# Layer norms inside an attention layer: the row scaling moved two pairs ahead of the transposes

## The chip, the cores and the metric

The kernel runs on one core of a Trainium2 chip. Its metric is the device time of one launch in microseconds (us), as the median of several runs. Engines are called as the profile calls them: PE is TensorE, with PEld for its weight loads; DVE is VectorE, ACT is ScalarE, POOL is GpSimd, and SP is SyncE, on whose queue the DMAs are issued.

## The reference, cut to what matters

Two layers work on 8 images of 256 channels and 32 x 32 positions. Layer 0 is a convolutional attention with a feed-forward part. Its output is read as 8 sequences of 1024 tokens with 256 channels each. Layer 1, where the change lies, is:

```python
t = _to_tokens(x)
t = t + _L1_attn_ref(_ln_t(t), WQ, WK, WV)
t = t + _L1_ffn_ref(_ln_t(t), ...)

def _ln_t(v, eps=1e-5):
    m = jnp.mean(v, axis=-1, keepdims=True)
    s = jnp.var(v, axis=-1, keepdims=True)
    return (v - m) / jnp.sqrt(s + eps)

def _L1_attn_ref(E, WQ, WK, WV):
    ...
    W = jnp.einsum('bqd,bkd->bqk', Q, K) / scale
    M = jnp.where(W == 0, jnp.zeros_like(W), tril[None, :, :])
    x_exp = jnp.exp(W - x_max) * M
    A = x_exp / (jnp.sum(x_exp, axis=-1, keepdims=True) + EPS)
    return jnp.einsum('bqk,bkd->bqd', A, V)
```

So every image passes two layer norms: a first one ahead of its attention and a second one behind it. The feed-forward part is a mixture of 8 experts; its gate reads the mean of the normed tokens over the images.

## The kernel before, in words

The launch has three stages: layer 0 (0 to some 1424 us), layer 1's attention (to some 2077 us), and the mixture of experts, called MoE here (to the end).

In layer 1 an image t[b] lies with its channels on the partitions, as two halves of 128 channels (KC = 2) by 1024 tokens. A norm over the channels needs tokens on the partitions, so `layer_norm` (L1287) turns the image, norms its rows, and turns them back. It works on n blocks of 128 tokens in pairs. For each pair PE makes four transposes into one PSUM bank `tpt`, ACT copies them to `zt`, and DVE takes mean and variance (`bn_stats`, `bn_aggr`) into `mv`. When all pairs are done, six small POOL operations make the factors `r`. Then `scaled(i0)` (L1317) subtracts the mean from the rows of a pair and multiplies them with r, in place, by two DVE operations (zt<-zt,mv,r). Four transposes (`tpz`) and one ACT copy per pair bring them back into `dst`. `zt` is one buffer for all blocks (bufs=1), so no pair waits for room of another.

The order of the instructions on each engine is the order of the program: all engines are called through `InOrder` (L60), which records every instruction at L72, so that L72 is the line of all of them in the profile. The program interleaves generators. `together(main, side, ratio)` (L446) runs main; at each step main yields its estimated time, and the side gets steps as long as the sum of what it has yielded is below 0.85 of main's sum. What is left of the side when main has ended runs after it. The number behind a `yield` thus decides only how many steps of the other generator stand between two pieces of work.

For each image b the main generator is `causal(b)` (L1527): for each of 8 rows of 128 queries, `scores` (L1543; s<-kk,z in two halves, on DVE the negated maximum `nm`, on ACT the exponential into `pr`), and then `follow` (L1532), which issues what became ready: a `product` (L1584; po<-pT,v, then t<-t,po on DVE), the `norm` of a former row (L1559; DVE: the lower triangle, the sum, the reciprocal rs; POOL: pr<-pr,rs), and from the third row on the `turn` of a former row (L1570; transposes tp<-ident,pr of up to four blocks into one bank, with an ACT copy into pT). The last rows of an image are turned during the next image's first scores.

The side is `beside(b)` (L1601), in this order: `first_norm(b + 1)`, the norm of the next image into z; three steps of `chores`, the experts' weights cut into parts (DVE: parts_w); `second_norm(b - 1)`, the norm of the image before into z2, with the sums for the gate on POOL (feat<-feat,z, in two halves), and `z_parts` (L1505), which cuts z2 in parts for the MoE stage (ACT: parts, DVE: parts<-z,parts and z<-parts) and stores them; two more chores; `keys_values(b + 1)` (L1465; pk on PE copied by ACT to kk, pv copied to v); two more chores. Beside the last image stand `last_norm` (L1516, n = 4) and the gate's first half in place of keys_values. The MoE stage calls `layer_norm` once more in `last_half` (L1820, n = 4), which advances by two steps in every second of its rounds.

The banks `tpt`, `tpz` and `tp` share one tag of the PSUM pool ps_t with two buffers (`bank`, L1455, and L1577 of `turn`): a tile of one of these kinds waits for the ACT copy of the tile two before it in that order. Scores have two buffers of their own (ps_s); pk, pv and po share two more (ps_m).

Of the kernel before, what the change touches and what calls it, by code (L numbers as in the profile page):

```python
# [104 lines left out]
def conv_attn_hybrid_kernel(  # L105
# [1181 lines left out]
    def layer_norm(src, dst, zt, room, bank):  # L1287

        n = src.shape[2] // P
        mv = room([P, NT, 2], "mv", 2)  # L1290
        for i0 in range(0, n, 2):
            tp = bank([P, 2, C], "tpt")
            for i in range(2):
                for k in range(KC):
                    c0 = (i0 + i) * P
                    pe.transpose(tp[:, i, k * P : (k + 1) * P], src[:, k, c0 : c0 + P], ident)
            act.copy(zt[:, i0 : i0 + 2, :], tp)
            yield 0.6
            for i in range(i0, i0 + 2):
                st = room([P, 6], "st", 4)  # L1300
                dve.bn_stats(st, zt[:, i, :])
                dve.bn_aggr(mv[:, i, :], st)
            yield 0.6

        y = room([P, NT], "y1", 2)[:, :n]
        r = room([P, NT], "r1", 2)[:, :n]
        pool.tensor_scalar(y, mv[:, :n, 1], LN_EPS, None, ALU.add)
        pool.tensor_tensor(r, y, mhalf1[:, :n], ALU.pow)
        pool.tensor_mul(y, y, r)
        pool.tensor_mul(y, y, r)  # L1310
        pool.tensor_scalar(y, y, -0.5, 1.5, ALU.mult, ALU.add)
        pool.tensor_mul(r, r, y)

        for _ in range(4):
            yield 1.0

        def scaled(i0):  # L1317
            for i in range(i0, i0 + 2):
                dve.tensor_scalar(zt[:, i, :], zt[:, i, :], mv[:, i, 0:1], r[:, i : i + 1], ALU.subtract, ALU.mult)

        scaled(0)
        yield 0.5
        for i0 in range(0, n, 2):
            if i0 + 2 < n:
                scaled(i0 + 2)
            tp = bank([P, KC, 2, P], "tpz")
            for i in range(2):
                for k in range(KC):
                    pe.transpose(tp[:, k, i, :], zt[:, i0 + i, k * P : (k + 1) * P], ident)
            act.copy(dst[:, :, i0 * P : (i0 + 2) * P], tp.rearrange("p k i c -> p k (i c)"))  # L1330
            yield 0.9
# [31 lines left out]
    with ExitStack() as l1:  # L1363
# [88 lines left out]
        def room(shape, tag, bufs):  # L1452
            return tiny.tile(shape, F32, tag=tag, name=tag, bufs=bufs)

        def bank(shape, name):  # L1455
            return ps_t.tile(shape, F32, tag="tp", name=name)
# [4 lines left out]
        def first_norm(b):  # L1461
            z[b] = two.tile([P, KC, N], F32, tag="z", name="z1")
            yield from layer_norm(t[b], z[b], rows_of_zt(), room, bank)
# [25 lines left out]
        def second_norm(b):  # L1489
            yield from until((b, N // QC - 1))  # L1490
            z2 = two.tile([P, KC, N], F32, tag="z2", name="z2", bufs=1)
            yield from layer_norm(t[b], z2, rows_of_zt(), room, bank)
            nc.sync.dma_start(u_d[b], t[b])
            if b + 3 < B:
                load_t(b + 3)
            for h, feat in enumerate(feats):
                half = z2[:, :, h * HALF : (h + 1) * HALF]
                if b == 0:
                    pool.tensor_copy(feat, half)
                else:  # L1500
                    pool.tensor_add(feat, feat, half)
            for h in range(2):
                yield from z_parts(b, h, z2[:, :, h * HALF : (h + 1) * HALF])
# [12 lines left out]
        def last_norm():  # L1516

            yield from until((B - 1, HALF // QC - 1))
            yield from layer_norm(t[B - 1][:, :, :HALF], z2_last, rows_of_zt(), room, bank)
            dve.tensor_add(feats[0], feats[0], z2_last)  # L1520
            nc.sync.dma_start(u_d[B - 1][:, :, :HALF], t[B - 1][:, :, :HALF])
            yield 0.5
# [459 lines left out]
```

## Time and profile before

| what | us |
|---|---|
| median of 3 runs | 3204.36 |
| lowest and highest of them | 3199.16, 3207.84 |
| the profiled execution, whole | 3211.16 |
| its span, first to last instruction | 3209.1 |
| PE busy (92% of the span) | 2950.3 |
| DVE busy (74%) | 2380.9 |
| ACT busy (49%) | 1568.7 |
| POOL busy (11%) | 342.7 |

The mean granted clock of PE was 0.964 of full speed. One profiled execution lies behind every duration given later; its own time is 6.8 us above the median. A line of the timeline or of the groups of instructions names the engine, the operation, its output and inputs by the program's names, the shapes (partitions x elements), how many of them (x4), and in brackets the engine's idle time just before it, with what ended it. The start of a line and its length come first, in us. In the page's groups the two numbers behind the bar are the busy us of the group and the mean ns of one instruction. PE's instructions overlap by their pipeline, so the length of one includes some of the next.

### The profile page before, as it was taken

The page shows a single profiled execution, that of the slowest core. Times are in us where ns is not written, and L with a number is a line of the kernel's source. Part 1 is how long each engine was busy: PE and PEld are TensorE (multiplying, and loading weights), DVE is VectorE, ACT ScalarE, POOL GpSimd, SP SyncE. Part 2 cuts the span into 40 slices and gives each one's busy share as a digit, 9 for nine tenths or more (in the row PEclk, how much of TensorE's full clock was granted, in tenths as well). Part 3 has the DMA queues.
Part 4 walks back from the last instruction along what each step waited for, and adds up shares of the span by engine and source line. Part 5 has one row for each costly group of instructions (what it writes and reads, how often), then busy time and mean ns, then how long its engine had stood idle before and what let it go on. Part 6 is the DMA issues. An engine that isn't in the chain of part 4 may idle for free. (4 is left out here: it accounts for less than half of the span.)

```text
span 3209.1 us, 41633 instructions
## 1 busy us (share of the span) xinstructions
PE 2950.3 (92%) x16802; PEld 1936.8 (60%) x16802; DVE 2380.9 (74%) x3014; ACT 1568.7 (49%) x2312; POOL 342.7 (11%) x419
## 2 busy tenths in 40 slices
PE   5998898998998989958999999899999999999998
PEld 3654545554555555535566556577777777777776
DVE  1378778778787879574766665588988898888888
ACT  1554444454554546313333333365666666666665
POOL 1121212111111110001222221100000000000000
PEclk9998999999999999979999999899999999999999
DMA  5213030302121110011433221231211242221220
GB/s 151 60 22 79 27 80 27 79 27 69 38 63 44 52 42 8 17 58 57 150 116 118 105 102 53 109 121 66 99 66 66 73 162 100 92 73 66 86 79 27
DMA packets 63854, 234.85 MB, mean 73 GB/s; under 512 B 5590, under 2 KB 13862, under 8 KB 54822
## 3 DMA queue, kind: packets, MB, share of 16 engines
q1 hardware_dynamic: 63654, 232.12, 21.7%
q8 instruction: 134, 2.20, 0.3%
q14 instruction: 66, 0.54, 0.1%
HBM read 140.61 MB, written 91.49 MB: 72 GB/s over the span
## 5 line engine op out<-in xcount | busy, mean ns | idle before, releaser
L72 PE MATMUL pa<-ze,w 128*128 128x512 f32 x1488 | 422.8, 392 | 0.0
L72 DVE SCALAR_TENSOR_TENSOR x<-hpad,vec,x 128x1024 f32<-128x1024 f32 x248 | 317.1, 1283 | 40.6 <-ACT x L72 33.5
L72 DVE SCALAR_TENSOR_TENSOR conv<-hpad,vec,conv 128x1024 f32<-128x1024 f32 x256 | 329.3, 1293 | 15.5 <-ACT conv L72 8.9
L72 PEld LDWEIGHTS pa<-ze,w 128*128 128x128 f32 x1488 | 277.9, 188 | 63.2 <-issue 3.3
L72 ACT ACTIVATE h<-pa,bn_o,s1a 128x512 f32<-128x512 f32 x256 | 198.8, 777 | 207.3 <-PE pa L72 207.3
L72 ACT ACTIVATE pT<-s 128x1024 f32<-128x1024 f32 x256 | 247.5, 1025 | 72.0 <-PE s L72 72.0
L72 PE MATMUL po<-pT,vT 128*32 128x256 f32 x4096 | 273.4, 385 | 0.0
L72 PE MATMUL q<-h2p,w 128*128 128x512 f32 x768 | 269.4, 459 | 0.1
L72 DVE SCALAR_TENSOR_TENSOR h<-pa,s1b,h 128x512 f32<-128x512 f32 x256 | 191.4, 748 | 95.6 <-PE pa L72 87.0
L72 PE MATMUL s<-kk,z 128*128 128x512 f32 x512 | 247.9, 614 | 1.0 <-DVE pr L72 1.0
L72 PE MATMUL ph<-xn,piw 128*128 128x512 f32 x512 | 244.6, 615 | 3.1 <-DVE xn L72 1.6
L72 PE MATMUL pm<-h,w 128*128 128x512 f32 x512 | 240.9, 593 | 0.0
L72 PE MATMUL q<-z_first,w 128*128 128x512 f32 x768 | 216.5, 390 | 2.8 <-DVE z_first L72 1.7
L72 PE MATMUL pm<-h1p,w 128*128 128x512 f32 x768 | 217.0, 391 | 0.5 <-DVE h1p L72 0.5
L72 DVE SCALAR_TENSOR_TENSOR o<-vpad,pe_w,o 128x1024 f32<-128x1024 f32 x128 | 163.5, 1282 | 45.9 <-ACT o L72 42.7
L72 PEld LDWEIGHTS q<-h2p,w 128*128 128x128 f32 x768 | 144.5, 188 | 83.8 <-issue 59.6
L72 PE MATMUL s<-qst,kst 128*128 128x256 f32 x1024 | 176.1, 314 | 14.9 <-DMA kst<-part 13.5
L72 ACT ACTIVATE hpad<-ph,pi_o 128x512 f32<-128x512 f32 x126 | 86.9, 690 | 183.6 <-PE ph L72 183.6
L72 PEld LDWEIGHTS po<-pT,vT 128*32 128x32 f32 x4096 | 120.6, 110 | 85.6 <-issue 3.9
L72 PEld LDWEIGHTS s<-qst,kst 128*128 128x128 f32 x1024 | 137.6, 193 | 48.1 <-issue 42.7
L72 PEld LDWEIGHTS q<-z_first,w 128*128 128x128 f32 x768 | 144.2, 188 | 34.5 <-DVE z_first L72 2.9
L72 PEld LDWEIGHTS pm<-h1p,w 128*128 128x128 f32 x768 | 144.6, 188 | 32.1 <-DVE h1p L72 0.9
(268 smaller groups left out, 5065.7 us busy)
## 6 DMA issues: line engine op xcount, KB each, us to landing
ze<-zd SPq DMA_DIRECT2D x29, 1536.0 KB, 6.4
qst<-part SPq DMA_DIRECT2D x32, 512.0 KB, 8.6
kst<-part SPq DMA_DIRECT2D x32, 512.0 KB, 15.1
te<-ud SPq DMA_DIRECT2D x32, 512.0 KB, 4.1
wd<-parts_w SPq DMA_DIRECT2D x20, 768.0 KB, 3.6
w<-wd SPq DMA_DIRECT2D x20, 768.0 KB, 4.3
zd<-parts SPq DMA_DIRECT2D x14, 1024.0 KB, 4.1
t<-in_x_dram SPq DMA_DIRECT2D x8, 1024.0 KB, 5.2
```

The costliest lines, as they stand in the source:

```text
L72: return self._tc.keep_in_program_order(method(*args, **kwargs))
```

## The change

Only the second part of `layer_norm` is changed:

```diff
         scaled(0)
-        yield 0.5
+        yield 1.0
+        scaled(2)
+        yield 1.0
         for i0 in range(0, n, 2):
-            if i0 + 2 < n:
-                scaled(i0 + 2)
+            if i0 + 4 < n:
+                scaled(i0 + 4)
             tp = bank([P, KC, 2, P], "tpz")
             for i in range(2):
                 for k in range(KC):
                     pe.transpose(tp[:, k, i, :], zt[:, i0 + i, k * P : (k + 1) * P], ident)
             act.copy(dst[:, :, i0 * P : (i0 + 2) * P], tp.rearrange("p k i c -> p k (i c)"))
             yield 0.9
```

Before, the first pair was scaled, the generator yielded 0.5, and each turn of the loop scaled the next pair and then transposed its own. After it, the first pair is scaled, the generator yields 1.0, the second pair is scaled, it yields 1.0 again, and each turn scales the pair two further on and then transposes its own. The instructions are the same ones; a norm's yields add up to 1.5 more than before, and there is one more of them. All calls of `layer_norm` are affected: the first and second norms of the 8 images, last_norm, and last_half.

## Prediction

> **What bounds the kernel now.** I read the page's first two parts first, for the engine shares.
>
> ```profile
> PE 2950.3 (92%) x16802; PEld 1936.8 (60%) x16802; DVE 2380.9 (74%) x3014; ACT 1568.7 (49%) x2312; POOL 342.7 (11%) x419
> ```
>
> PE is busy 92% of the span. That is a mean over three stages, so the stage with the changed function was read alone. The changed code runs in layer 1's attention (about 1424 to 2077 us) and once, thinly spread, in the MoE stage. The table of windows for 80 us of the attention (columns: window, length, busy PE, PEld, DVE, ACT, POOL, clock, DMA share, GB/s):
>
> ```profile
> 1680.00:1760.00 80.00, 74.40 (x306) 47.67 (x305) 52.60 (x124) 27.40 (x48) 18.00 (x22) 0.98 0.34 131
> ```
>
> PE again 93%, DVE 66%, DMA a third: PE sets the pace, and a gap in PE is time. The waits from 1500 to 2000 us (six and a half images; columns: total us, times, longest) say where the gaps are:
>
> ```profile
> PE tpz L72 <- DVE zt L72: 21.6, 27, 1.5
> ...
> PE tp L72 <- ACT pT L72: 3.5, 6, 0.6
> PE pk L72 <- ACT kk L72: 2.1, 3, 0.7
> PE tp L72 <- ACT zt L72: 2.0, 6, 0.3
> ...
> PE tpz L72 <- ACT z L72: 1.4, 6, 0.2
> ```
>
> The norms' transposes (tpz) waiting for their scaled rows (zt) are the largest, some 3.3 us an image. The chain of waits at the end of the page covers only the last 37% of the span and is no help here. So I went through PE's timeline of one image. The first norm (of the next image):
>
> ```profile
> 1689.58 1.88 PE L72 MATMUL s<-kk,z 128*128 128x512 f32 x4
> 1692.31 0.67 PE L72 MATMUL tpz<-ident,zt 128*128 128x128 f32 x4 [0.85 <-DVE zt L72]
> ...
> 1695.80 0.66 PE L72 MATMUL tpz<-ident,zt 128*128 128x128 f32 x4 [0.24 <-ACT z L72]
> 1697.05 0.66 PE L72 MATMUL tp<-ident,pr 128*128 128x128 f32 x4 [0.59 <-ACT pT L72]
> ...
> 1699.70 0.59 PE L72 MATMUL s<-kk,z 128*128 128x512 f32 x1
> ```
>
> And the second norm (of the image before):
>
> ```profile
> 1719.01 3.60 PE L72 MATMUL s<-kk,z 128*128 128x512 f32 x8
> 1723.81 0.41 PE L72 MATMUL tpz<-ident,zt 128*128 128x128 f32 x2 [1.20 <-DVE zt L72]
> 1724.54 1.08 PE L72 MATMUL tpz<-ident,zt 128*128 128x128 f32 x6 [0.32 <-DVE zt L72]
> ...
> 1730.06 0.41 PE L72 MATMUL tpz<-ident,zt 128*128 128x128 f32 x2 [1.54 <-DVE zt L72]
> 1730.89 0.44 PE L72 MATMUL tpz<-ident,zt 128*128 128x128 f32 x2 [0.42 <-DVE zt L72]
> 1731.16 3.15 PE L72 MATMUL s<-kk,z 128*128 128x512 f32 x4
> 1734.11 3.66 PE L72 MATMUL po<-pT,v 128*128 128x256 f32 x16
> ```
>
> Records overlap, so I count from start to start: half a row of scores (4 records) holds PE 1.72 us, a tpz bank (4 transposes) 0.43, one tp transpose 0.11. The first norm's section runs from 1689.58 to about 1701.42 (1699.70 + 1.72), 11.84 us. Its work is 4 x 1.72 + 4 x 0.43 + 8 x 0.11 = 9.48, so 2.4 us are lost; the same section at 1535.71 to 1547.84 loses 2.65. The second norm's runs from 1719.01 to 1734.11, 15.1 us for 6.88 + 1.72 + 0.44 = 9.04 of work, so 6.1 are lost: 4.8 in waits, some 1.3 in the 3.15 us that the scores took instead of 1.88.
>
> [...] the windows of PE at the same place one image earlier show it busy all the time at half clock,
>
> ```profile
> 1651.00:1653.00 2.00, 2.00 (x3) 0.50 0.00 0
> ```
>
> behind some 3.3 us with only transposes and waits. It comes about once an image. [...] for zt: 0.40 us alone, but its pair below takes 1.31 beside POOL's scaling of pr (1729.78 for 0.91, POOL's timeline):
>
> ```profile
> 1729.52 1.31 DVE L72 TENSOR_SCALAR zt<-zt,mv,r 128x256 f32<-128x256 f32 x2
> ```
>
> **The change, part by part.** No instruction is added or removed; the 96 zt of 483 ns, the transposes and the copies stay. Two scaled pairs stand ahead of the first tpz instead of one, and the generator yields 2.0 instead of 0.5 ahead of it: 1.5 more of main's steps. The rows are in one zt buffer of all 8 blocks, so two pairs ahead need no room.
>
> *First norm, 7 times (images 1 to 7).* VectorE's order at its start is as before: six zt in a row, then nm(1). PE's becomes: both halves of scores(1), tpz0, tp of row 7 (two banks), half of scores(2), tpz1, tpz2, the other half, tpz3, po(3). Scores(1) 1689.58 to 1693.02. The zt end about 1693.8, but the first pair is ready at 1692.2: tpz0 to 1693.45, no wait. The second tp bank needs tpz0's bank, whose copy (588 ns) ends about 1694.25: a stall of 0.4. Then scores to 1696.4. The pT copies stand behind exp(1) on ACT, which waits for nm(1) (1.22, to 1695.1), and end at 1696.2 and 1696.8, as tpz1 and tpz2 want them. Scores to 1699.0, tpz3, po(3) at 1699.5 where it was 1701.42. Gain 1.9; with the section at 1535 it is 2.26. I take 2.1: 7 x 2.1 = 14.7 us. Ends: 1.5 and 2.4 (all of it).
>
> *Second norm, 7 times beside attention (images 0 to 6).* PE before: scores(5), tpz0, tpz1, tp(3), half of scores(6), tpz2, tpz3, other half, po(2). After: scores(5), tp(3), half of scores(6), tpz0, tpz1, other half, tpz2, tpz3, po(2). Removed: the 1.20 + 0.32 ahead of tpz0, since tp(3) starts at 1722.5 and scores(6) runs to 1724.8 over the zt. Added: tpz1 takes the bank of tp(3), whose copy stands on ACT behind exp(5); that waits for nm(5), now 1725.0 to 1726.2 behind four zt; exp 0.90, copy 0.58: 1727.8, a stall of 2.55. Queued behind tpz1 on PE is the other half of scores(6), and nm(6) waits for that. It ends 1729.9. The last two scaled pairs come after norm(5), where POOL scales pr (0.91) and then adds feat, which the trace has at
>
> ```profile
> L72 POOL TENSOR_TENSOR feat<-feat,z 128x1024 f32<-128x1024 f32 x10 | 23.5, 2367 | 0.0
> ```
>
> Its first half needs only z0 and z1 and can now start near 1730.05. [...] the last zt end at 1732.7 and po(2) starts at 1733.2; if zt get in first, at 1731.3. Before it was 1734.11 in images with the half clock here, 1732.88 in the others, mean 1733.5. So +0.3 or +2.2. Behind it VectorE's and ACT's chain to exp(7) and the keys is nearly as late (the third pk started at 1745.69 or 1744.86, by my count 1744.75 after), so little of the better end passes on. Matmul-free stretches are 3.5 and 3.2 us long (before 3.75 and 3.24), so I keep one half-clock phase an image[...]. I take +0.4, ends -1.0 and +1.6: 7 x 0.4 = 2.8 us.
>
> *Last image and end.* In image 7, nm(7) no longer stands behind parts and z (1.22 us each) on VectorE, so the wait of po(5) at 2045.9 (5.3 us) shrinks by up to 3. At the end, last_norm's second tpt moves into the last po, and its chain of stats 1.15, POOL 2.5 and zt reaches its tpz some 2 us later. Together +1, ends -2 and +3.
>
> *Moved without price.* The side's sum grows by 3.0 an image, to about 59 against the 41.4 that main lets through, so more of keys_values runs after main; it did so before, PE-dense there, nothing lost. The DMA issues behind the second norm (u, t(b+3), parts) shift by under 3 us on SP's queue; t(b+3) is wanted two images later. POOL's factors r stand ahead of all this. In the MoE stage the norm has n=4 and one yield more, so the second gate comes one slot later, long before its use: 0.
>
> *Sum:* 14.7 + 2.8 + 1 = 18.5 us. The profiled run took 3211.16 (span 3209.1 and 2.1 around it): 3192.7. It lies 6.8 above the median of the runs, 3204.36, which gives 3186.
>
> **Rivals.** A difference under 0.3% (9.6 us) can hardly be told from none here.
> 1. *Likeliest, 0.45:* as summed, 13 to 25 us gained, 3179 to 3191, 3186.
> 2. *The second norm gains too, 0.15:* [...] the half-clock phase goes. 14.7 + 7 x 1.6 + 1 + some half-clocks (up to 7 x 1.3) is 27 to 36: 3172. The trace's 28.5 us of waits listed above are the ceiling but for the clock. Against: nearly equal stretches.
> 3. *The gain is given back in part, 0.26:* the second norm loses 1 us each (7), the first gains 1.5 (10.5), the end loses 2: 1.5 us; up to 13 with milder losses. 3197.
> 4. *Slower, 0.14:* [...] the other three wait 2.4 us, tpz2 as well as tpz3 is late, po(2) stands at 1733.8. The stretch is then 3.9 us[...]: 2.0 late. The second feat then blocks parts' subtraction (2.22 beside feat, 1.22 alone, at 1657.8): 3.0 in all. 7 x (2.1 - 3.0) - 2 = -8.3: 3213. It decides from 2.1 us of loss per second norm. For it: zt's 1.31 above. Against: VectorE issues its four zt back to back, and the path wants only the last.
>
> **How the numbers follow.** Faster by over 0.3%: 0.45 + 0.15 + 0.06 of case 3 = 0.66. Within: 0.20 of case 3 and 0.02 of case 4 = 0.22. Slower: 0.12. The range is 3169 to 3208: below lies 0.05, above some 0.12.
>
> **What would show it.** Right: PE's waits for zt in the first norm near 0, a new wait of about 0.4 of tp for z, an image period some 2 us shorter (76.8 now), PE busy time unchanged. In the second norm a wait of tpz for pT of about 2.5, then one for zt under 2.7. Wrong: a stretch at half clock on po(2) in each image, zt pairs at over 2 us, or scores waiting for nm(1) in the first norm.

## The result, and the profile after

The changed kernel takes 3189.32 us (median of 6 runs, 3185.13 to 3194.78); the kernel before took 3206.98 in the 6 runs beside it. The ratio is 0.9947, with a 95% interval of 0.9937 to 0.9957: some 17 us faster, where 18.5 was worked out. For each experiment the kernel before was measured again (medians 3204.5 to 3206.9), and each ratio below is against those runs.

The profiled execution of the changed kernel took 3188.79 us, its span 3186.8. That is 22.3 less than the profiled one before, but not all of it is the change's: layer 0 ended 3.0 us earlier, with the same code. From PE's last operation ahead of layer 1 (votes) to the gate's first matmul (lg) it was 641.9 us before and 621.1 after. From there to the end 1143.2 and 1144.7.

PE's waits from 1500 to 2000 us, after (total us, times, longest; lines of other engines left out):

```profile
PE tpz L72 <- ACT pT L72: 13.6, 6, 2.3
...
PE tpz L72 <- DVE zt L72: 5.2, 4, 2.0
...
PE tp L72 <- ACT zt L72: 2.0, 6, 0.3
...
PE tp L72 <- ACT z L72: 1.4, 6, 0.2
...
PE tpz L72 <- ACT z L72: 0.8, 1, 0.8
PE pk L72 <- ACT kk L72: 0.5, 3, 0.2
```

The 21.6 us of waits for zt have become 5.2, and a new wait of 13.6 has come, six times 2.27: tpz for the bank of tp(3), which the pT copy frees. The sum of PE's waits went from 31.0 to 23.5. PE's timeline of a first norm, after:

```profile
1528.15 3.60 PE L72 MATMUL s<-kk,z 128*128 128x512 f32 x8
1531.59 0.60 PE L72 MATMUL tpz<-ident,zt 128*128 128x128 f32 x4
1532.03 0.60 PE L72 MATMUL tp<-ident,pr 128*128 128x128 f32 x4
1532.86 0.66 PE L72 MATMUL tp<-ident,pr 128*128 128x128 f32 x4 [0.24 <-ACT z L72]
1533.36 1.88 PE L72 MATMUL s<-kk,z 128*128 128x512 f32 x4
1535.08 1.04 PE L72 MATMUL tpz<-ident,zt 128*128 128x128 f32 x8
1535.95 1.88 PE L72 MATMUL s<-kk,z 128*128 128x512 f32 x4
1537.67 0.60 PE L72 MATMUL tpz<-ident,zt 128*128 128x128 f32 x4
1538.11 6.65 PE L72 MATMUL po<-pT,v 128*128 128x256 f32 x32
```

From 1528.15 to 1538.11 it takes 9.96 us for 9.48 of work; only the wait for tpz0's bank is left. And a second norm:

```profile
1703.29 3.60 PE L72 MATMUL s<-kk,z 128*128 128x512 f32 x8
1706.72 0.60 PE L72 MATMUL tp<-ident,pr 128*128 128x128 f32 x4
1707.39 1.95 PE L72 MATMUL s<-kk,z 128*128 128x512 f32 x4
1709.18 0.60 PE L72 MATMUL tpz<-ident,zt 128*128 128x128 f32 x4
1712.05 0.67 PE L72 MATMUL tpz<-ident,zt 128*128 128x128 f32 x4 [2.27 <-ACT pT L72]
1712.54 3.58 PE L72 MATMUL s<-kk,z 128*128 128x512 f32 x4
1715.93 0.63 PE L72 MATMUL tpz<-ident,zt 128*128 128x128 f32 x4
1716.95 0.67 PE L72 MATMUL tpz<-ident,zt 128*128 128x128 f32 x4 [0.40 <-DVE zt L72]
1717.46 3.20 PE L72 MATMUL po<-pT,v 128*128 128x256 f32 x16
```

The wait of 1.20 ahead of the first tpz is gone; 2.27 ahead of the second has taken its place. The section, from scores(5) to po(2), takes 14.17 us. Its half row of scores at 1712.54 runs at half clock, as the windows show (columns: window, length, PE busy, clock, DMA share, GB/s; the clock is 0.50):

```profile
1713.00:1715.00 2.00, 2.00 (x3) 0.50 0.00 0
```

Behind it the last rows arrive late. VectorE's four zt, and POOL's work beside them:

```profile
1713.15 3.98 DVE L72 TENSOR_SCALAR zt<-zt,mv,r 128x256 f32<-128x256 f32 x4
1717.05 1.21 DVE L72 TENSOR_REDUCE nm<-s 128x1 f32<-128x1024 f32 x1
```

```profile
1713.40 0.91 POOL L72 TENSOR_SCALAR pr<-pr,rs 128x768 f32<-128x768 f32 x1 [4.79 <-DVE rs L72]
1714.28 2.38 POOL L72 TENSOR_TENSOR feat<-feat,z 128x1024 f32<-128x1024 f32 x1
```

Four zt of 0.40 take 3.98 us. feat runs from 1714.28 to 1716.66, and only then do the last zt end.

So a second norm now has three delays on top of one another (bank, half clock, feat), and two of them hide each other. Image 1's second norm, from 1628.98, has no half clock (1.00 all along): its tpz2 stands 1.7 us earlier in the section, tpz3 waits the longer for zt,

```profile
1639.95 0.70 PE L72 MATMUL tpz<-ident,zt 128*128 128x128 f32 x4
1642.64 0.67 PE L72 MATMUL tpz<-ident,zt 128*128 128x128 f32 x4 [2.00 <-DVE zt L72]
```

and the section takes the same 14.17 us.

By section, in the profiles, over six images each (first norm of images 2 to 7, second norm of images 0 to 5; the third column runs from po(2) to the first pv, and holds 14.54 us of work):

| kernel | first norm | second norm | po(2) to pv |
|---|---|---|---|
| before | 11.84 to 12.13 | 13.87 and 15.1 in turn | 15.0 and 15.5 in turn |
| after | 9.95 to 9.99 | 13.53, then 14.17 | 14.5 to 15.0, once 16.2 |

The 15.1 are the second norms whose last half row of scores runs at half clock (in the 13.87 a phase falls earlier, beside waits); the 16.2 is the one image of the changed kernel in which such a phase fell on po(2). The first norms of images 2 to 7 give 11.6 us, the second norms of images 0 to 5 2.5, the third column 0.9. The beginning of layer 1 gives 4.6: 2.7 of them in image 1's first norm, where a phase at half clock went as well, and 1.2 in the transposes and keys ahead of it, which began at half clock before and which the edit does not touch. The rest of the 20.8, some 1.3, is in the last image.

### The profile page after: what moved, and what is told of

Same layout as the page of the kernel before. It is cut to its first block, busy times and chain, and to the rows that moved or that the text cites. A ratio compares the mean times of both kernels' runs of the same rounds, so it can differ in the third digit from the quotient of the medians.

```text
span 3186.8 us, 41632 instructions
## 1 busy us (share of the span) xinstructions
PE 2936.5 (92%) x16802; PEld 1934.3 (61%) x16802; DVE 2390.5 (75%) x3014; ACT 1567.0 (49%) x2312; POOL 340.3 (11%) x419
## 4 chain that ended last, share of the span: by engine, by line
PE 46%; DVE 6%; ACT 2%; issue 1%; DMA 0%; POOL 0%; SPq 0%; ACTq 0%; DVEq 0%; POOLq 0%
PE pm L72 12%; PE pa L72 11%; PE q L72 11%; PE s L72 4%; PE po L72 3%; PE pv L72 2%; PE pk L72 1%; DVE nm L72 1%; DVE zt L72 1%; DVE pr L72 1%; ACT pr L72 1%; PE tpz L72 1%; PE tpt L72 1%; DVE st L72 1%; PE tp L72 1%
## 5 line engine op out<-in xcount | busy, mean ns | idle before, releaser
L72 PE MATMUL s<-kk,z 128*128 128x512 f32 x512 | 241.3, 603 | 1.0 <-DVE pr L72 0.6
## 6 DMA issues: line engine op xcount, KB each, us to landing
kst<-part SPq DMA_DIRECT2D x32, 512.0 KB, 15.1
```

The lines of the kernel that those rows point to most:

```text
L72: return self._tc.keep_in_program_order(method(*args, **kwargs))
```

## The experiments

My theory after this, A: the gain is made in the first norms; in the second norms new waits eat most of what the old ones cost. Rivals: the second norms carry half (B); the scaling ahead does it rather than the delay (C); the bank is what limits a second norm (G).

**First norms alone.** A flag gives `first_norm` the new form and leaves the others in the old one:

```diff
-            yield from layer_norm(t[b], z[b], rows_of_zt(), room, bank)
+            yield from layer_norm(t[b], z[b], rows_of_zt(), room, bank, True)
```

> The change in the first norms alone; second norms, last_norm and last_half as before. Theory A (the gain is made in the first norms, some 1.9 us in each of images 2 to 7 and 2.7 in image 1, by leaving no transpose in front of its scaled rows): 12 to 15 us faster than before, all but a few us of the whole change. Rival B (the second norms carry half of it): 7 to 9 us faster.

Measured: 3190.51, ratio 0.9949 (0.9935 to 0.9963), 16 us. First norms take 9.95 us, as in the change. A bit above the numbers of A, and its interval, 12 to 21 us, holds them; B's lie outside.

**Second norms alone.** The same flag at `second_norm`.

> The change in the second norms alone (8 of them), all else as before. Theory A: a second norm gains 0.4 us in the mean, since the waits for zt that go come back as a wait for the bank of tp(3) and one for zt behind POOL's feat: 0 to 6 us faster, 3 likeliest. Rival B: 7 to 10 us faster.

Measured: 3202.99, ratio 0.9997 (0.9988 to 1.0005), nothing to be told. The low end of A; B is out. The two parts together (0.51% and 0.03%) make the change's 0.53%. The profile shows the second norms at 14.17 us (the first at 13.53), as in the change, but in three images of six a phase at half clock falls on po(2), and the stretch from po(2) to pv takes 16.2 us instead of 15.0. Over the six images the sections gained 2.5 us, and that stretch lost 1.6 again.

**The delay without the scaling ahead.**

```diff
         scaled(0)
         yield 1.0
-        scaled(2)
         yield 1.0
         for i0 in range(0, n, 2):
-            if i0 + 4 < n:
-                scaled(i0 + 4)
+            if i0 + 2 < n:
+                scaled(i0 + 2)
```

> The yields as in the change (1.0 and 1.0), but rows scaled only one pair ahead, as before. Theory A (in a first norm the delay alone does it: PE has two halves of scores ahead of the first transpose, and the third pair, scaled behind norm(1), is ready when its transposes are due): first norms as in the change, second norms 1 us worse than in the change (the second pair now stands behind norm(5) on VectorE, its transposes wait for it): 8 to 15 us faster than before, 11 likeliest. Rival C (scaling two ahead is what frees PE): 0 to 5 us faster.

Measured: 3190.43, ratio 0.9954 (0.9941 to 0.9968), 15 us. First norms 9.95 us: as A has it, and C is out. In the first norms the delay is the change. The second norms are at 15.13 (one at 15.85), 1.0 above the change, and there the second tpz waits 3.27 us for its scaled pair. But all six also have a phase at half clock behind that wait, where nothing hides it: in the one from 1704.79 half a row of scores takes 2.84 us from start to start instead of 1.72, and eight tpz 1.43 instead of 0.87. So the 1.0 is not the price of the later pair alone; what the second scaled pair is worth by itself is not shown.

**The scaling ahead without the delay.**

```diff
         scaled(0)
-        yield 1.0
         scaled(2)
-        yield 1.0
+        yield 0.5
```

> Rows scaled two pairs ahead, but with a single yield of 0.5 as before, so PE's order is that of before and VectorE does all eight zt in a row. Theory A: in the first norms nothing (the transposes wait for the first pair and for banks, as before); in a second norm the waits of 1.54 and 0.42 for zt behind norm(5) go, and pT's bank is waited for some 0.8 instead: 1.5 to 2 us each, in all 8 to 16 us faster, 13 likeliest. Rival D (without the delay the scaling ahead is worth nothing, since new waits take its place): 0 to 3 us faster.

Measured: 3206.49, ratio 1.0008 (1.0001 to 1.0014). My 13 us did not come; D has the number. But the sections show that D's place is wrong: the first norms are as before (11.83), and the second norms did shrink, to 12.26 us, by 1.6 to 2.8 as expected (one is at 13.18). What grew is the stretch behind them, from po(2) to pv: 15.0, 16.5, then 18.8 to 19.1 us, up to 4 more. Its timelines, of PE, VectorE and POOL:

```profile
1731.03 3.60 PE L72 MATMUL pk<-z,at 128*128 128x512 f32 x8
1737.20 5.12 PE L72 MATMUL pk<-z,at 128*128 128x512 f32 x8 [2.58 <-ACT kk L72]
```

```profile
1724.70 2.10 DVE L72 TENSOR_TENSOR parts<-z,parts 128x1024 f32<-128x1024 f32 x1
1726.89 3.22 DVE L72 SCALAR_TENSOR_TENSOR z<-parts 128x1024 f32<-128x1024 f32 x1
```

```profile
1723.37 5.65 POOL L72 TENSOR_TENSOR feat<-feat,z 128x1024 f32<-128x1024 f32 x2
```

PE waits for the keys' copy, which stands on ACT behind exp(7), which waits for nm(7), which stands on VectorE behind parts and z<-parts. Those took 2.10 and 3.22 us beside feat, where they take 1.22 and 1.23 alone. Behind the wait of 2.58 comes a phase at half clock, in four images of six: the last eight pk take 4.96 us from start to start instead of 3.44. This gave theory E: feat on POOL takes the gain back. Rival F: another wait does.

**The same without feat.**

```diff
                 if b == 0:
                     pool.tensor_copy(feat, half)
-                else:
-                    pool.tensor_add(feat, feat, half)
```

> The kernel with two pairs ahead and the single yield of 0.5, and with POOL's sums feat left out for all images but the first (so the gate's features of the others are missing). Theory E (that kernel gained 1.6 to 2.8 us in each second norm and lost it again some 12 us later, because feat started earlier, [...] and so held nm(7), exp(7) and the copy of the keys, for which pk waited 2.6 us): the gain comes through, 8 to 15 us faster than before, 11 likeliest. Rival F (the loss comes from another wait, or PE gives it back elsewhere): within 3 us of before.

This kernel leaves out the sums of seven images, so it only measures what they cost. Measured: 3186.73, ratio 0.9941 (0.9928 to 0.9953), 19 us. F is out; behind every image whose sums are left out the stretch from po(2) to pv is 14.54, all work. The gain is above E's numbers: I had left out the 0.7 us that this stretch already wasted before, and the phases at half clock, of which the six images show two instead of six.

**feat moved, nothing left out.** First norms as in the change, the other norms with two pairs ahead and the short yield. `z_parts` used to overwrite z2, so feat had to read it first; here its low part goes into the rows of zt, which are dead by then, and feat stands behind `z_parts` (lines left out at the dots):

```diff
+                low = zt[:, h * NT // 2 : (h + 1) * NT // 2].rearrange("p (k i) c -> p k (i c)", k=KC)
-                yield from z_parts(b, h, z2[:, :, h * HALF : (h + 1) * HALF])
+                yield from z_parts(b, h, z2[:, :, h * HALF : (h + 1) * HALF], low)
...
-            dve.scalar_tensor_tensor(src, parts[:, 1], -STEP, parts[:, 0], ALU.mult, ALU.add)
+            dve.scalar_tensor_tensor(low, parts[:, 1], -STEP, parts[:, 0], ALU.mult, ALU.add)
```

> First norms as in the change; second norms, last_norm and last_half with two pairs ahead and the single yield of 0.5; the low part that z_parts makes goes to the dead rows of zt instead of over z2, and POOL's sums feat stand behind z_parts. Nothing is left out. Theory E: both gains add, 20 to 31 us faster than before, 26 likeliest. Rival F: 11 to 17 us faster, as the first norms alone.

Measured: 3173.39, ratio 0.9899 (0.9885 to 0.9913), 32 us, a bit above E's 31: the fastest kernel of this study. First norms 9.95 but for one at 10.39, second norms 12.26 in four of six, po(2) to pv 14.54 in all. VectorE and POOL there:

```profile
1716.99 1.22 DVE L72 TENSOR_TENSOR parts<-z,parts 128x1024 f32<-128x1024 f32 x1
1718.24 1.23 DVE L72 SCALAR_TENSOR_TENSOR zt<-parts 128x1024 f32<-128x1024 f32 x1
...
1732.97 2.46 DVE L72 TENSOR_SCALAR parts_w<-parts_w 128x512 fp32r<-128x512 f32 x1
```

```profile
1729.60 5.54 POOL L72 TENSOR_TENSOR feat<-feat,z 128x1024 f32<-128x1024 f32 x2
```

POOL still holds VectorE up: a parts_w of 0.43 us now takes 2.46. But nothing of PE waits for parts_w there. The first norm at 10.39 is the exception: parts_w, so held, and the transfer behind it (4.3 us of waiting at 1667.35) stand ahead of its statistics.

**That kernel with feat where it was.** The same edit without the moved feat and without `low`.

> First norms as in the change; second norms, last_norm and last_half with two pairs ahead and the single yield of 0.5, feat where it was. Theory E: the first norms' gain alone, 11 to 18 us faster than before. Rival F (what the second norms lost depends on the first norms' order): over 20 us faster.

Measured: 3192.51, ratio 0.9953 (0.9941 to 0.9965), 15 us, as E has it: second norms of 12.27 to 13.20, and 14.5 to 19.1 from po(2) to pv. The two kernels differ by 16.5 us in that stretch over the six images. Some 3 of these are half clock, which falls into two of the stretches here (18.8 and 19.1 us, against 17.4 with the same wait of 2.58 and full clock) and into none where feat is moved. Feat and the low part's place were moved together, so their shares are not told apart.

**The change with a bank of its own for the second norms' tpz.** They take a bank of the pool of pk, pv and po:

```diff
+        def bank_m(shape, name):
+            pool_, tag = (ps_m, "mm") if name == "tpz" else (ps_t, "tp")
+            return pool_.tile(shape, F32, tag=tag, name=name)
...
-            yield from layer_norm(t[b], z2, rows_of_zt(), room, bank)
+            yield from layer_norm(t[b], z2, rows_of_zt(), room, bank_m)
```

> The change, with the second norms' transposes in the pool of banks that pk, pv and po use, so that they don't wait for the copy of tp(3). Theory A: the wait of 2.3 us goes, but the last scaled rows are still held to the same time by POOL's feat[...]: 8 to 18 us faster than before, no better than the change itself and perhaps some us worse. Rival G (the bank is what the second norms lost): 26 to 32 us faster than before.

Measured: 3197.38, ratio 0.9970 (0.9962 to 0.9979), 10 us: worse than the change by some 8. PE's timeline of a second norm:

```profile
1710.82 1.88 PE L72 MATMUL s<-kk,z 128*128 128x512 f32 x4
1714.45 0.41 PE L72 MATMUL tpz<-ident,zt 128*128 128x128 f32 x2 [1.75 <-DVE zt L72]
...
1717.71 1.09 PE L72 MATMUL tpz<-ident,zt 128*128 128x128 f32 x4 [1.75 <-DVE zt L72]
```

The wait for the bank is gone, and the time is waited for zt instead: the section takes 14.55 us. The stretch with only transposes and waits, from 1712.54 to po(2) at 1718.59, is longer, and at its end the profile has the half clock (0.51 from 1715 to 1718 us; 6.8 us of it in three images of six). From po(2) to pv PE has no wait, yet the stretch takes 14.7 to 17.1 us for 14.54 of work: what is over is half of the time at half clock that falls into it (2.4 of 4.8 us, 2.5 of 5.1). It is 5.6 us more than in the change over the six images, most of the 8. A as expected; G is out.

**The change in all norms with feat moved.**

> The change in all norms, with z_parts' low part in the dead rows of zt and POOL's feat behind z_parts. Theory E (in the change feat holds the last scaled rows of a second norm until 2.4 us later, behind which the wait for tp(3)'s bank and the half clock stand): the second norms' sections shrink from 14.2 us to 12 to 13.5, and the stretch from po(2) to pv to about 14.6: 23 to 33 us faster than before, 26 likeliest. Rival F (feat only fills time that other waits take anyway): 14 to 20 us faster, as the change.

Measured: 3182.86, ratio 0.9930 (0.9916 to 0.9943), 22 us, a bit under E's 23, its interval 18 to 27. The second norms are at 12.14 us (one at 13.44) instead of 14.17. The last four zt, which took 3.98 us beside feat in the change, take 1.95 here; that with what hung on it cost 2.0 there, and po(2) to pv is at 14.7. But three first norms are at 11.47. In one of them the trace shows how: feat now meets parts_w (2.57 and 2.73 us for two of them, 0.43 and 0.69 alone), the next parts_w, behind them, waits 5.0 us for its weights on VectorE, and this norm's own statistics stand in line behind it:

```profile
1665.62 0.43 DVE L72 TENSOR_SCALAR parts_w<-we 128x512 fp32r<-128x512 f32 x1 [5.00 <-DMA we<-in_wo_dram]
...
1667.88 0.42 DVE L72 BATCH_NORM_STATS2 st<-zt 128x6 f32<-128x256 f32 x1
```

The wait as such is not new: the changed kernel has it too (5.07 us at 1665.77) with a first norm of 9.95, which starts 3 us later there (1675.74 against 1672.59). So E holds for the second norms; of what they gained, a part was lost at this new place. Of half clock the six images have one phase here and five in the changed kernel, so a part of the gain is the clock's.

**The kernel before with feat moved.**

> The kernel before, with z_parts' low part in the dead rows of zt and POOL's feat behind z_parts, and nothing of the change. Theory E (before, feat started behind the last transposes and was over when parts began, so it cost almost nothing there; it costs only where the rows are ready earlier): 0 to 4 us faster than before. Rival H (feat's place alone makes the gain of the version with both): 9 us or more faster.

Measured: 3200.04, ratio 0.9987 (0.9980 to 0.9993), 4 us, at E's upper end. H is out.

## Why the prediction was right

It gave 18.5 us; 17 were measured. Its largest term and the path behind it were right; that the sum came so near is in part luck, as the steps show:

- *First norms.* 2.1 us each were taken, with the order and the one wait that would be left (0.4 expected; the section is 0.48 above its work). The profiles give 2.18 once, 1.85 to 1.89 five times, and 2.7 in image 1, half-clock phase included: 14.3 in sum, where 14.7 was taken. The first-norms-only kernel shows that this is nearly all.
- *What does it there.* The prediction followed PE's order and did not part the two halves of the edit. The delay alone gives the first norms' gain: with half a row of scores more ahead of the first transpose, the rows were ready whether one pair or two had been scaled.
- *Second norms.* +0.4 each was taken. The profiles give 0.42 in the mean, and the steps are as written: a stall of 2.27 at the second tpz (2.55 worked out), the zt behind feat, po(2) at the worse of its two times. On the chip, the second norms alone were worth 0.03%, within its interval of nothing. Half-clock phases, one an image by the prediction's estimate from the lengths of the stretches without matmuls, came in five of the six images. Four fell on a second norm, where feat hides them as shown above, and one on po(2). That was luck: with the second norms alone changed, three fell on po(2), at some 1.2 us each.
- *The last image and the end.* +1 was taken. The wait ahead of po(5) fell from 5.31 to 2.96 us, and a phase at half clock that stood on po(5) before (24 of them took 6.58 us, now 5.03) is gone, which no step had; last_norm's transposes gave 2.3 back in new waits (1.76 and 0.57); some 1.3 is left at lg. The MoE stage took 1.5 us longer in the profiled runs, which is less than layer 0 differs between them.
- *The rivals.* What the fourth was about, feat holding up the second norm's zt, was there: four of them took 3.98 us beside it. It did not decide: what it cost was no more than the waits for zt that had gone. Its 2.0 us of delay at po(2) was an estimate; a phase at half clock there cost 1.2 (16.2 against 15.0). In the kernel with the scaling ahead only it did decide, at another place, behind the norm. The prediction had named that bite (feat against parts), at 1.0 us; parts and z<-parts together show 2.9 more, and the stretch behind the norm up to 4, of which some 1.5 is half clock.

My own expectation of the mechanism failed once, with that kernel: I followed the second norm to its end and not on to nm(7), the next consumer on VectorE. Four other numbers missed their ranges: 16 us for 12 to 15, 19 for 8 to 15, 32 for 20 to 31, and 22 for 23 to 33.

The half clock was not tested by itself, and it moves with every edit. What a phase costs can be read where one kernel has the same section with and without it: nothing in the changed kernel's second norms (14.17 us both), 0.9 in the second norms of the kernel with feat moved (13.12 and 13.19 against 12.26), 1.2 on the changed kernel's po(2) (16.2 against 15.0), and 1.4 to 1.7 in the stretch behind the norm with feat left in place (18.8 and 19.1 against 17.4).

## What to carry to other kernels

Where PE is the bound and its queue is in program order, an instruction that waits can be placed later, or its input made earlier. Here the first paid at once: one step of other work ahead of the transposes gave 15 us. Scaling earlier gave nothing in sum by itself, but 19 us with POOL's sums left out. So follow a gain to the next instruction that waits on each engine: here 2 us gained in a norm were lost some 12 us later, since the gain brought POOL's sums against VectorE's critical operations. POOL work that holds VectorE up (here feat, beside which parts and z<-parts took 5.32 us in place of 2.45) is best moved to where VectorE has nothing urgent; with the scaling ahead in the second norms that was worth another 17 us (32 against 15, a few of them the clock's), while a free bank made the change 8 us slower.

## What the runs showed of the hardware

In the traces of the kernel before and of the changed one, all phases at half clock (0.50 granted) start on one grid of 3.413 us: counted from the first instruction, their starts have the same remainder by 3.413 (to 0.01 us), 1.07 us for the 37 phases of the kernel before and 2.48 for the 34 of the changed one. Their lengths are multiples of 3.413 us, but for the last phase of each trace: 3.41 among the images from 1500 to 1960 us, and up to 27.31 where layer 1 begins.

Among these images 11 phases begin in the two traces. In the 3.413 us of the grid just ahead of each, PE was busy by the records with matmuls other than transposes for 0.00 to 0.90 us, so a stretch wholly without matmuls was not needed. But three such stretches of the kernel before with 0.58 to 0.62 us of them, from 1540.5, 1694.1 and 1847.7, had no half clock behind them; what else decides stays open.

Phases need not keep step with the images. With periods of 77.4, 76.4, 77.2 us before, the phases came after 71.7 and 81.9 us in turn, 21 and 24 steps of the grid; in the changed kernel, with periods of 73.2 to 75.8 us, they came after 146.8, 75.1, 78.5 and 71.7. The six images show six phases before, five in the changed kernel, two in the kernel with feat moved. So a saving of 2 us at one place can go with a phase more or less at another, and a comparison of two kernels holds some of it.

Where feat met VectorE's work in the kernel with the scaling ahead only, both took longer: z<-parts 3.22 us (1.23 without feat, in the kernel with feat moved), and the two sums of feat 5.65 (4.69 in the kernel before).
